# Two graph layers on one core: the order of work where layer two begins is changed

## The chip, the core and the metric

One core of a Trainium2 chip runs the whole program in one launch. The core has five engines that run their own instruction streams and meet at semaphores: TensorE (PE, matrix products and transposes), VectorE (DVE), ScalarE (ACT), GpSimd (POOL) and SyncE (SP), which here only issues DMAs. The metric is the device time of one execution in microseconds; lower is better. The kernel before took 3624.22 us (median of 3 runs, 3620.76 to 3637.07).

## The reference, cut to what matters

There are N = 2708 nodes with D = 512 features, and a dense adjacency matrix `adj` of N x N zeros and ones.

```python
# layer one: normalise, clear, graph attention with 8 heads of 64, add
h = relu(layernorm(x))
x = x + relu(gat(h, adj))
# layer two: normalise, clear, two diffusion steps, add
X = relu(layernorm(x))
S = adj + I;  Rf = S / rowsum(S);  Rb = S / colsum(S)[:, None]
Xf = Xb = Xa = X;  Z = 0
for s in range(2):
    logits = Xa @ W1 @ W2 @ (Xa @ W3).T          # N x N
    A = softmax(logits, only the largest entries of a row that reach mass 0.9)
    Xf = Rf @ Xf;  Xb = Rb @ Xb;  Xa = A @ Xa
    Z = Z + Xf @ U1[s] + Xb @ U2[s] + Xa @ U3[s]
out = x + layernorm(X + Z)
```

In step one (s = 0) Xf and Xb are still both X, so one product with S serves both: S.T-tiles times X, scaled by row sums for Xf and by column sums for Xb. In step two they differ.

## The kernel before

**Tiles.** The 2708 nodes are 22 tiles of 128 rows, the last of 20 rows. Tiles go in 11 pairs (G = 2; the text calls a pair also a group), in 6 quads, and the columns of a row of logits in 6 chunks of 452. `early_tiles` is 18: the tiles ahead of the last two pairs.

**Layer one** (lines 202 to 464) works through six column blocks of adj. For each block and head, DVE makes a masked weight tile `e` (L440) and PE multiplies it (L442). A block's tiles are then finished by `finished`, in stages: turn the heads' sums (L351), share them out, normalise, clear (`v`, L390), and `asked`: transpose v (L397), project it to keys and queries (`project`, L160, which writes kq_d through POOL), and split v into two parts for exact products (`split_rows`, which writes vhl_d through POOL). Stages of earlier blocks are threaded through the next block's loop; those of the last three tiles (19, 20, 21) come at the very end, with nothing beside them. Here `rest` also writes `xb_d`, the input of the last sum. While layer one runs, S is written to DRAM as `s_d`. After layer one some small tiles are set up, among them `ones`, `across` and `below_d` (L500 to L505, the pool `ramps`), on the addresses that layer one has left, and after them the pool `big` on the same base, with `va` (the values X, 22 tiles) and `keys`.

**Layer two, step one**, is the loop over s = 0 from L950. From L1235 on the order of PE, ACT, DVE and SP is the order of the program (`manual_schedule`), so each of these engines works strictly through its list; POOL's order is made by a scheduler. Per pair of tiles:

- `Logits.queries` loads q, `Logits.products` makes two rows of logits p (L536 on PE, L538 copies by ACT). p has 4 buffers: two pairs.
- `Logits.exp` holds the maxima (L564, DVE), two exponentials a tile on ACT, and six looks a tile (ACT passes over p that measure the mass above a guess, L571).
- `search` (DVE) finds the cut for mass 0.9: passes over p (L650), then `finish` (L844, L846, L779), which writes the kept weights `keep` and a flag that picks a branch (L928). `early` and `late` are hooks: what is called there stands at that place in each engine's list. `early` begins with the outstanding `pending` splits and the next pair's maxima.
- `attended` (PE) transposes keep (L1096), ACT copies it (L1100), and PE multiplies it with va (L1118). Its twelve steps take work from two lists: `fills` (ACT's passes for a later pair) and `others` (a part of S's block).
- `mixed` multiplies with U3 (L1158) and projects for step two (L160).

**S's blocks.** `part(half, b)` gives the steps of half a block for one quad: an even b is 22 `product` steps (load hl of vhl_d, 512 KB, and s_r of s_d, 256 KB, then eight matmuls, L1012); an odd b is `across` (four copies to `tt`, also stored as tt_d for step two), then four `through` steps with U1 (L1030, each loads a u_k) and a `scaled` that puts x tiles on the list `pending` for `split_rows` to fhl_d, and the same with U2 for bhl_d. hl, s_r and u_k have 3 buffers each.

**The opening before.** SP loads keys in two pieces (L965), then q; PE makes the logits of pair 0; then all of part 0 (22 products); then va is loaded (L976). For g = -1: part 1 and pair 1's logits, while DVE searches pair 0. From g = 0 on, phase g holds part g + 2, pair g + 2's logits, the attention of pair g and the search of pair g + 1. Parts end with part 11, so phase 10 of step one has none. At g = 0 the ACT passes left over from the opening (`looks`) are threaded into `attended` first.

**Step two** has the same loop with its own parts (L1009), which also load tt_d back (L1000).

Of the kernel before, what the change touches and what calls it, by code (L numbers as in the profile page):

```python
# [53 lines left out]
def kernel(  # L54
# [41 lines left out]
    const = ctx.enter_context(tc.tile_pool(name="const", bufs=1))  # L96

# [104 lines left out]
    with ExitStack() as l0:  # L202
# [133 lines left out]
        def finished(t, o_t, c0, bank, final):  # L336
# [48 lines left out]
            def cleared():  # L385
                _, o, mean, rs = held
                v = work.tile([P, D], F32, name="v", bufs=3)
                held.append(v)
                nc.vector.tensor_scalar(o[:pr], o[:pr], mean, rs, op0=OP.subtract, op1=OP.mult)
                nc.scalar.activation(v[:pr], o[:pr], AF.Relu)  # L390
                nc.gpsimd.dma_start(out=va_d[cols[t], :], in_=v[:pr])

            def asked():
# [6 lines left out]
                if not final:  # L400
                    split_rows(halves, nc.gpsimd, v[:pr], t, vhl_d)
                project(halves, bank(1), v_t, t, 0, bufs=TG)

            def rest():
                split_rows(halves, nc.vector, held[4][:pr], t, vhl_d)
                with_beta(held[0])

            return [turned, shared, normed, cleared, asked] + [rest] * final

        later = {}  # L410
        for ci, tiles in enumerate(tchunks):
# [95 lines left out]
    class Logits:  # L507
# [20 lines left out]
        def products(self):  # L528
            wide, small, ps_l = self.pools
            for q, t in zip(self.q, self.grp):  # L530
                pr = rows[t]
                p = wide.tile([P, N], F32, name="p", bufs=4)
                for c0, c1 in chunks:
# [5 lines left out]
                self.p.append(p)  # L539
# [402 lines left out]
    big = ctx.enter_context(tc.tile_pool(name="big", bufs=1))  # L942
    va = big.tile([P, NT, D], F32, name="va")

    keys = big.tile([P, N], F32R, name="keys")
# [4 lines left out]
    for s in range(STEPS):  # L950
        last = s == STEPS - 1
        with ExitStack() as st:
# [5 lines left out]
            small = st.enter_context(tc.tile_pool(name=f"s{s}small", bufs=2, reuse_waits="tile"))  # L958
            ps_t = st.enter_context(tc.tile_pool(name=f"s{s}pst", bufs=2, space=PSUM, reuse_waits="tile"))
            ps_a = st.enter_context(tc.tile_pool(name=f"s{s}psa", bufs=2, space=PSUM, reuse_waits="tile"))  # L960
            ps_s = st.enter_context(tc.tile_pool(name=f"s{s}pss", bufs=1, space=PSUM, reuse_waits="tile"))

            def asked(s, c):
                for i in range(2):
                    nc.sync.dma_start(out=keys[i * DA:(i + 1) * DA, c].bitcast(F32), in_=kq_d[s][:DA, i, c])  # L965

            if not last:
                asked(s, slice(0, early_tiles * P))
            asked(s, slice(early_tiles * P, N))
            if last:  # L970
                also = st.enter_context(tc.tile_pool(name="s1also", bufs=1))
            rank = also.tile([P, N], BF16, name="rank") if last else None

            def values(queue):
                for t in range(NT):
                    queue.dma_start(out=va[:rows[t], t, :], in_=(xa_d if last else va_d)[cols[t], :])  # L976

# [4 lines left out]
            def part(half, b):  # L982
# [12 lines left out]
                def product(c):  # L995
                    if c == 0:
                        half[:] = [ps_s.tile([P, D], F32, name=f"q{i}") for i in range(len(quad) if last else KD)]
                        if last and first:
                            across_t.append(work.tile([P, KD, 2 * G * P], F32, name="tt", bufs=1))
                            nc.sync.dma_start(out=across_t[-1][:, :, :w], in_=tt_d[b // 2][:, :, :w])  # L1000
# [14 lines left out]
                def across():  # L1015

                    tt = work.tile([P, KD, 2 * G * P], F32, name="tt", bufs=1)
                    for k in range(KD):
                        nc.scalar.copy(tt[:, k, :w], half[k][:, :w])
                    nc.gpsimd.dma_start(out=tt_d[b // 2][:, :, :w], in_=tt[:, :, :w])  # L1020
                    across_t.append(tt)

                def through(u, k, start):
# [5 lines left out]
                    for j in range(len(quad)):  # L1029
                        nc.tensor.matmul(half[j], lhsT=across_t[-1][:, k, j * P:(j + 1) * P], rhs=u_k,  # L1030
                                         start=(start and k == 0), stop=(start and k == KD - 1))

                def scaled(inv, to, now):

                    paced(pending, len(pending))
                    for j, t in enumerate(quad):
                        pr = rows[t]
                        x = work.tile([P, D], F32, name="xe", bufs=4)
# [31 lines left out]
                for u, inv, to, now in ((u1[1], rinv, fhl_d, b > 1), (u2[1], cinv, bhl_d, False)):  # L1070
                    steps += [lambda k=k, u=u: through(u, k, True) for k in range(KD)]
                    steps.append(lambda inv=inv, to=to, now=now: scaled(inv, to, now))
# [162 lines left out]
            with tc.manual_schedule(engines={PE, ACT, DVE, SP}):  # L1235
                junk = wide.tile([P, -(-N // 4) * 2], F32, name="junk", bufs=1)
                lg = [Logits(pools, s, grp, keys, rank) for grp in pairs[:1]]
                lg[0].queries()
                lg[0].products()
                steps = lg[0].exp(looks=False)  # L1240
                counts = []
                if last:
                    values(nc.gpsimd)
                    heads, counts = ranked(junk.bitcast(BF16)[:, :N], list(range(early_tiles, NT)), "keep", 2)
                    paced(heads, len(heads))
                for step in lg[0].maxima + steps + counts:
                    step()
                half = []
                lg += [Logits(pools, s, grp, keys, rank) for grp in pairs[1:2]]
                lg[1].queries()  # L1250
                others = part(half, 0)
                if last:
                    paced(others, NT // 2)
                    spread()
                    lg[1].products()
                paced(others, len(others))
                if not last:
                    values(nc.sync)
                done = []
                ready = None  # L1260
                looks, left = [], []
                for g in range(-1, NP):
# [3 lines left out]
                    others = part(half, g + 2)  # L1266
                    if g + 2 < NP and not (last and g < 0):
# [106 lines left out]
```

## Time and profile before

| | us |
|---|---|
| median of 3 runs | 3624.22 |
| the profiled execution | 3630.61 |
| its span | 3628.7 |
| PE busy | 3334.1 (92% of the span) |
| DVE busy | 2652.9 (73%) |
| ACT busy | 1505.5 (41%) |
| layer one's last L442 matmul ends | 1051.8 |
| first logits of layer two begin (L536) | 1089.4 |
| group 2's logits resume (L536) | 1221.6 |
| step two's products begin (L1009) | 2342.5 |

All durations and instants in this text are those of the profiled execution, counted from the start of its span, and its own time is 6.4 us above the median of the runs. In a row of the time line the first two numbers are start and length; a bracket at the end tells how long the engine stood idle before it and what released it. A row of the waits reads: who waited, for whom, us in total, times, longest.

### The profile page before, as it was taken

The numbers are of one execution on the slowest core, as the hardware profiler recorded it, in microseconds if no ns is written. First come the engines' busy times: TensorE is split into PE (matmuls) and PEld (weight loads), VectorE is DVE, ScalarE is ACT, GpSimd is POOL, SyncE is SP. The second block draws the span as 40 slices with busy tenths as digits, with TensorE's granted clock in tenths as the row PEclk, the third lists the DMA queues.
The fourth block names the chain that finished last, engine by engine and source line by source line (L and its number), as shares of the span: only waits on it lengthen the run. The fifth ranks groups of instructions, "written<-read, shape, count | busy, mean of one in ns | idle before, by whom it ended". The sixth has DMA issues, their size and how long they took to land. (4 is left out here: it accounts for less than half of the span.)

```text
span 3628.7 us, 34073 instructions
## 1 busy us (share of the span) xinstructions
PE 3334.1 (92%) x10797; PEld 1718.8 (47%) x10797; DVE 2652.9 (73%) x4828; ACT 1505.5 (41%) x2269; POOL 854.2 (24%) x1054
## 2 busy tenths in 40 slices
PE   7999999998967789999999999889999999999877
PEld 4433333333444454555546454355555555555433
DVE  4587888889975455546365463598889988889984
ACT  2344212011103566656465662335545654455610
POOL 4114241515321021122222221221112212122211
PEclk9999999999989889999999999999999999999989
DMA  3477424232218352534445253574556445565433
GB/s 114 150 242 246 149 89 143 75 118 94 94 59 283 116 186 90 211 108 163 160 151 192 95 205 109 172 275 159 201 186 231 151 164 203 185 224 191 160 119 132
DMA packets 247956, 579.99 MB, mean 160 GB/s; under 512 B 33305, under 2 KB 67049, under 8 KB 243491
## 3 DMA queue, kind: packets, MB, share of 16 engines
q1 hardware_dynamic: 226695, 503.59, 41.4%
q0 software_dynamic: 21040, 73.88, 5.3%
q8 instruction: 86, 1.41, 0.2%
q14 instruction: 135, 1.11, 0.1%
HBM read 471.68 MB, written 105.68 MB: 159 GB/s over the span
## 5 line engine op out<-in xcount | busy, mean ns | idle before, releaser
L1118 PE MATMUL a<-va,at 128*128 128x512 f32 (+2 forms) x1936 | 893.6, 601 | 8.4 <-ACT at L1100 8.3
L442 PE MATMUL po<-e,fw 128*65 128x512 f32 (+4 forms) x2112 | 842.7, 554 | 30.7 <-DVE e L440 21.7
L440 DVE SCALAR_TENSOR_TENSOR e<-r_b,kk,a_c 128x512 f32<-128x512 f32 (+4 forms) x1056 | 750.8, 739 | 71.6 <-PE po L442 21.6
L571 ACT ACTIVATE junk_a<-p,nth 128x2708 uint8<-128x2708 f32 (+1 forms) x240 | 612.7, 2553 | 57.8 <-POOL nth L586 53.5
L1009 PE MATMUL q<-hl,s_r 128*128 128x512 f32 x1936 | 525.9, 420 | 66.9 <-DMA s_r<-s_d 65.1
L442 PEld LDWEIGHTS po<-e,fw 128*65 128x65 f32 (+1 forms) x2112 | 286.9, 140 | 546.6 <-issue 270.9
L1118 PEld LDWEIGHTS a<-va,at 128*128 128x128 f32 (+2 forms) x1936 | 340.3, 187 | 381.1 <-issue 336.5
L1009 PEld LDWEIGHTS q<-hl,s_r 128*128 128x128 f32 x1936 | 363.1, 191 | 219.7 <-issue 59.7
L650 DVE SCALAR_TENSOR_TENSOR junk<-p,th 128x2708 bf16<-128x2708 f32 (+1 forms) x132 | 424.6, 3217 | 3.3
L1100 ACT COPY at<-t 128x512 f32<-128x512 f32 (+3 forms) x308 | 140.0, 476 | 503.9 <-PE t L1096 499.6
L1030 PE MATMUL q<-u_k,tt 128*128 128x512 f32 x704 | 318.6, 595 | 10.3 <-DMA u_k<-in_L_gnn_U_dram 10.3
L1012 PE MATMUL q<-s_r,hl 128*128 128x512 f32 (+1 forms) x1056 | 280.6, 410 | 11.6 <-DMA s_r<-s_d 11.3
L538 ACT COPY p<-t 128x452 f32<-128x452 f32 (+2 forms) x264 | 130.8, 536 | 382.6 <-PE t L536 332.8
L1012 PEld LDWEIGHTS q<-s_r,hl 128*128 128x128 f32 x1056 | 186.7, 188 | 99.6 <-issue 51.5
L1030 PEld LDWEIGHTS q<-u_k,tt 128*128 128x128 f32 x704 | 134.1, 191 | 160.8 <-issue 145.7
L536 PE MATMUL t<-keys,q_t 128*128 128x452 f32 x528 | 155.5, 419 | 58.6 <-ACT p L538 45.4
L564 DVE TENSOR_REDUCE nmx<-p 128x1 f32<-128x2708 f32 (+1 forms) x44 | 130.6, 2968 | 104.4 <-ACT p L538 104.4
L846 DVE MAX8 vn<-keep 128x8 f32<-128x2708 f32 (+1 forms) x66 | 196.8, 2981 | 2.3
L424 ACT ACTIVATE s_c<-a_c 128x512 fp32r<-128x512 f32 (+3 forms) x132 | 76.2, 577 | 249.5 <-DMA a_c<-in_adj_t_dram 122.0
L1096 PE MATMUL t<-ident,keep 128*128 128x128 f32 (+1 forms) x968 | 147.8, 275 | 29.4 <-DVEq L933 13.9
L1096 PEld LDWEIGHTS t<-ident,keep 128*128 128x128 f32 (+1 forms) x968 | 115.0, 140 | 121.8 <-issue 86.6
L1158 PE MATMUL a<-u_k,v_t 128*128 128x512 f32 (+1 forms) x352 | 168.4, 615 | 1.8 <-DMA u_k<-in_L_gnn_U_dram 1.5
(312 smaller groups left out, 3308.2 us busy)
## 6 DMA issues: line engine op xcount, KB each, us to landing
s_r<-s_d SPq DMA_DIRECT2D x330, 256.0 KB
hl<-vhl_d SPq DMA_DIRECT2D x132, 512.0 KB
hl<-fhl_d SPq DMA_DIRECT2D x132, 512.0 KB
hl<-bhl_d SPq DMA_DIRECT2D x132, 512.0 KB
u_k<-in_L_gnn_U_dram SPq DMA_DIRECT2D x184, 256.0 KB
arow<-in_adj_dram SPq DMA_DIRECT2D x21, 1354.0 KB
s_d<-s_c SPq DMA_DIRECT2D x88, 256.0 KB
a_c<-in_adj_t_dram SPq DMA_DIRECT2D x84, 256.0 KB
```

Source lines behind the costliest of these rows:

```text
L440: nc.vector.scalar_tensor_tensor(e[:pr, :cw], r_b[:pr, i, :cw], kk[:pr, t, hd:hd + 1], a_c[t][:pr, :cw], op0=OP.max, op1=OP.mult)
L442: nc.tensor.matmul(po[i][:, :cw], lhsT=fw[:pr, t, hd, :], rhs=e[:pr, :cw], start=(t == 0), stop=(t == NT - 1))
L536: nc.tensor.matmul(pl[:, :c1 - c0], lhsT=q[:, i], rhs=self.keys[:, c0:c1], start=(i == 0), stop=(i == 1))
L571: nc.scalar.activation(junk[:pr], self.p[i][:pr], func, **kw)
L650: nc.vector.scalar_tensor_tensor(self.junk_b[:pr], p, th, p, op0=OP.is_ge, op1=OP.mult, accum_out=dst)
L846: v.max(vs, keep[0][:pr])
L1009: nc.tensor.matmul(half[j], lhsT=s_r[:, j * P:(j + 1) * P], rhs=hl[:, h], start=(c == 0 and h == 0), stop=(c == NT - 1 and h == 1))
L1012: nc.tensor.matmul(half[j][:, :w], lhsT=hl[:, h, j * P:(j + 1) * P], rhs=s_r[:, :w], start=(c == 0 and h == 0), stop=(c == NT - 1 and h == 1))
L1030: nc.tensor.matmul(half[j], lhsT=across_t[-1][:, k, j * P:(j + 1) * P], rhs=u_k, start=(start and k == 0), stop=(start and k == KD - 1))
L1096: nc.tensor.transpose(pt[:rows[c], j, :pr], keep[i][:pr, cols[c]], ident[:pr, :pr])
L1118: nc.tensor.matmul(pa[:pr], lhsT=at[:rows[c], j, :pr], rhs=va[:rows[c], c, :], start=(c == 0), stop=(c == NT - 1))
L1158: nc.tensor.matmul(pz[i][:rows[t]], lhsT=v_t[i][:, k, :rows[t]], rhs=u_k, start=(k == 0), stop=(k == KD - 1))
```

## The change

What it does, in the order of the program:

1. A pool `turn` with four 2 KB tiles named `v` is opened first. Layer one's v comes from it, and later the four parts of `tt`, which become tiles of their own; tt_d is written and read in four DMAs, one for each part.
2. The last three tiles of layer one are no longer projected and split there. They are put on a list `unasked`.
3. `big` waits tile by tile instead of for whole pools, and `keys` is its first tile. In the step's pools the PSUM of S's products is taken first.
4. Step one opens with three products of part 0. Then, three times: a third of the first 18 tiles' keys (SP), one product, and the split, transposition and projection of one of the unasked tiles. The keys of the last tiles are loaded by POOL's queue.
5. The logits of pair 0 come in two parts, the five chunks that need no late keys first, with three products between them and the last chunk. Then 9 products, pair 1's logits, the last 4 products, part 1 with the loads of va between its steps, and the whole of part 2.
6. From then on phase g holds part g + 3 instead of g + 2, so phases 9 and 10 have none. The splits of part 1 are held back until after the first search, and the ACT passes of pair 1 are all issued in the opening, instead of being threaded through phase 0.
7. Step two keeps its order; only the four tt tiles and the pools concern it.

The diff, cut to its core:

```diff
+    turn = ctx.enter_context(tc.tile_pool(name="turn", bufs=4, reuse_waits="tile"))
...
-                v = work.tile([P, D], F32, name="v", bufs=3)
+                v = turn.tile([P, D], F32, name="v")
...
-                if not final:
-                    split_rows(halves, nc.gpsimd, v[:pr], t, vhl_d)
-                project(halves, bank(1), v_t, t, 0, bufs=TG)
+                split_rows(halves, nc.gpsimd, v[:pr], t, vhl_d)
+                project(halves, bank(1), v_t, t, 0, bufs=2)
             def rest():
-                split_rows(halves, nc.vector, held[4][:pr], t, vhl_d)
                 with_beta(held[0])
-            return [turned, shared, normed, cleared, asked] + [rest] * final
+                unasked.append((t, held[4]))
+            return [turned, shared, normed, cleared, rest if final else asked]
...
-        def products(self):
+        def products(self, cs=chunks):
...
-    big = ctx.enter_context(tc.tile_pool(name="big", bufs=1))
+    big = ctx.enter_context(tc.tile_pool(name="big", bufs=1, reuse_waits="tile"))
+    keys = big.tile([P, N], F32R, name="keys")
     va = big.tile([P, NT, D], F32, name="va")
-    keys = big.tile([P, N], F32R, name="keys")
...
-            if not last:
-                asked(s, slice(0, early_tiles * P))
-            asked(s, slice(early_tiles * P, N))
...
-                            across_t.append(work.tile([P, KD, 2 * G * P], F32, name="tt", bufs=1))
-                            nc.sync.dma_start(out=across_t[-1][:, :, :w], in_=tt_d[b // 2][:, :, :w])
+                            across_t.append([turn.tile([P, D], F32, name="v") for _ in range(KD)])
+                            for k, tt in enumerate(across_t[-1]):
+                                nc.sync.dma_start(out=tt[:, :w], in_=tt_d[b // 2][:, k, :w])
...
-                    paced(pending, len(pending))
+                    if b > 1:
+                        paced(pending, len(pending))
...
+                    paced(others, 3)
+                    for n, (t, v) in enumerate(unasked):
+                        asked(s, slice(n * early_tiles // len(unasked) * P, (n + 1) * early_tiles // len(unasked) * P))
+                        paced(others, 1)
+                        split_rows(parts, nc.vector, v[:rows[t]], t, vhl_d)
+                        v_t = transposed(up, ps_t, v, rows[t], "v_t")
+                        project(small, ps_t.tile([P, 512], F32, name="t"), v_t, t, s)
+                    asked(s, slice(early_tiles * P, N), nc.gpsimd)
+                    lg[0].queries()
+                    lg[1].queries()
+                    ahead = [c for c in chunks if c[1] <= early_tiles * P]
+                    lg[0].products(ahead)
+                    paced(others, 3)
+                    lg[0].products(chunks[len(ahead):])
+                    steps = lg[0].exp(looks=False)
+                    for step in lg[0].maxima + steps:
+                        step()
+                    paced(others, 9)
+                    lg[1].products()
+                    paced(others, len(others))
+                    others = part(half, 1)
+                    loads = values(nc.sync)
+                    while others:
+                        paced(others, 1)
+                        paced(loads, 2)
+                    others = part(half, 2)
+                    paced(others, len(others))
...
-                    others = part(half, g + 2)
-                    if g + 2 < NP and not (last and g < 0):
+                    if last or g >= 0:
+                        others = part(half, g + 2 if last else g + 3)
+                    if 0 <= g < NP - 2:
                         lg[g + 2].products()
...
-                            paced(pending, len(pending))
+                            if g >= 0:
+                                paced(pending, len(pending))
...
+                        paced(fills, len(fills))
                         if last:
-                            paced(fills, len(fills))
                             paced(others, len(others))
-                        else:
-                            paced(others, 1)
-                            paced(fills, 2 * G + 1)
-                            while others:
-                                paced(others, KD + 1)
-                                paced(fills, G)
-                        looks.extend(fills)
...
+                        if g < 0 and not last:
+                            paced(pending, len(pending))
```

## The prediction

> **What bounds the kernel now.** I read the page first: engine totals and the forty slices. The profiled execution took 3630.61 us, with a span of 3628.7; slices of 90.7 us.
>
> ```profile
> PE 3334.1 (92%) x10797; PEld 1718.8 (47%) x10797; DVE 2652.9 (73%) x4828; ACT 1505.5 (41%) x2269; POOL 854.2 (24%) x1054
> ...
> PE   7999999998967789999999999889999999999877
> ...
> PEclk9999999999989889999999999999999999999989
> ```
>
> TensorE (PE) is busy nearly everywhere; the hole is in slices 12 to 14, from about 1000 to 1360 us, where layer two begins. The busy time by stretch, cut where PE's work changes kind, is the second view (stretch, length, busy time of each engine, granted clock, DMA share, GB/s):
>
> ```profile
> 1052.00:1089.40 37.40, 9.04 (x60) 7.63 (x58) 18.66 (x48) 4.52 (x13) 19.75 (x32) 0.55 0.41 124
> 1089.40:1153.50 64.10, 52.85 (x201) 36.35 (x202) 36.77 (x63) 17.10 (x22) 6.75 (x9) 0.97 0.85 294
> 1153.50:1171.40 17.90, 6.59 (x26) 3.60 (x24) 13.38 (x18) 13.93 (x23) 0.66 (x1) 0.82 1.01 364
> ...
> 1201.90:1221.60 19.70, 0.00 (x0) 0.00 (x0) 14.78 (x42) 5.63 (x6) 0.00 (x0) 0.61 0.07 29
> ...
> 1449.60:1558.90 109.30, 107.80 (x391) 66.15 (x390) 65.36 (x142) 60.39 (x74) 26.23 (x32) 1.00 0.62 219
> 1558.90:1659.50 100.60, 96.12 (x278) 46.10 (x276) 47.84 (x103) 65.03 (x83) 14.87 (x30) 0.97 0.24 83
> 2173.40:2249.00 75.60, 74.58 (x229) 36.02 (x227) 36.87 (x77) 15.67 (x35) 13.93 (x22) 1.00 0.34 110
> ```
>
> The first four rows are the transition. The last three are pair phases of step one: 96 to 99% PE, with VectorE (DVE) at 65 or less. So in step one PE is the bound, its work only moves, and the change is worth the PE idle time that it removes between 1052 and 1450. Third view, what PE's matmuls waited for from 1052 to 1222:
>
> ```profile
> PE t L536 <- ACT p L538: 20.8, 6, 19.8
> PE t L536 <- DMA q_t<-kq_d: 12.5, 1, 12.5
> PE po L397 <- ACT v L390: 12.1, 1, 12.1
> PE q L1012 <- DMA s_r<-s_d: 10.9, 14, 1.4
> PE q L1030 <- DMA u_k<-in_L_gnn_U_dram: 10.3, 1, 10.3
> PE po L160 <- ACT v_t L399: 3.7, 3, 2.6
> ```
>
> That is 70 us, each line one cause: layer one's last normalisation, the key and query round trip, S's products short of data, u_k queued behind va, and group 2's logits waiting for buffers that DVE's search of group 0 holds. After 1222 two waits follow, of 8.4 us (1281, the row below) and 6.3 us (1344, behind ScalarE's looks), and about 2 us is lost after each long one to a halved clock. Call it 95 us. The fourth view is the order of time:
>
> ```profile
> 1094.91 2.97 DVE L564 TENSOR_REDUCE nmx<-p 128x1 f32<-128x2708 f32 x1 [9.85 <-ACT p L538]
> ...
> 1221.06 0.17 DVE L939 RECIPROCAL rden<-den 128x2 f32<-128x2 f32 x1 [3.64 <-DVEq L928]
> ...
> 1289.34 1.12 PE L1096 MATMUL t<-ident,keep 128*128 128x128 f32 x4 [8.36 <-ACT v_t L149]
> ```
>
> The search of group 0 takes 126.2 us between the first two rows. 12.4 of it is a wait for group 1's logits; 22 (1171.3 to 1193.4) is S's first `split_rows`, queued ahead of `finish` and waiting for `xe`. Without them it takes 92. The last view is the SP queue's own waits:
>
> ```profile
> SPq L965 <- DVE below_d L505: 76.5, 1, 76.5
> ```
>
> SP could have issued long before. It stood at the first key load until 1071.9, because `big` lies where the ramps' tiles lay.
>
> **Part by part: the start.** After the last transposes (1054.2) PE now goes to S's products. Their SBUF lies under layer one's last e tiles, free with the last matmul at 1051.8; 4 us from issue to use (bounds: tt's 3.2 at least, and 4.5 for the first product of before, issue 1093.4 to start 1097.9) puts product 0 at 1056. One product loads 786 kB; 22 took 55.6 us, 2.53 each, or 311 GB/s. Products 0 to 2 end at 1063.
>
> Next on SP is the first piece of keys. With keys first in `big`, it still lies on the ramps' tiles, tile-by-tile waits or not, and L505 depends on the same normalisation as before. I keep 1072. Behind it on SP stand product 3's loads and all later ones; who waits is PE. The Trainium skill, "DMA: Bandwidth & Descriptors", section "Anatomy of one DMA", says that a semaphore wait happens on the issuing sequencer ahead of dispatch. That speaks against this order: product 3 has nothing to do with keys, yet stands behind them. The row of 76.5 us is such a standing queue. By the rule, product 3 has its data at 1078 (issue 1073.5, 4.5 more beside 0.39 MB of keys), 15 us of idle PE; were the queue to flow, the data would be there at 1066 and everything below comes 12 us sooner. I take the rule.
>
> Then three rounds of a key piece, a product and a projection. PE per round: a product 1.9, four transposes 0.7, the v_t copy 0.6 with its hand-over, eight L160 1.1, some of it at half clock: 5 us, 1094 at the end. DVE's three splits (1.1 each) and the POOL work were there before. The third key piece goes on POOL's queue behind kq_d's writes (3.1 us median to land): keys complete at about 1105. Meanwhile PE does ten chunks of logits (8.8 for twelve: 7.3; 1101.5) and products 6 to 8 (1107); the two last chunks end at 1108.5. **The search of group 0 so starts at 1108, 13 us later than before.**
>
> Products 9 to 17 are short of data (2.53 each against 1.9 of PE): 1129. Group 1's logits, 8 us: 1137, before DVE asks for them at 1108 + 50 = 1158. Products 18 to 21: 1145. Across, four copies: 1147.5. The two through-passes, 29.7 before with 2 us of half clock, plus 1 for eviction: 1176; u_k and va, 0.8 MB a step of 3.6 us, now alternate and hide, so the 10.3 us wait goes.
>
> **Block 2 in the opening.** 22 products more, three preloaded: 7 us, 18 × 2.53 and 2 at the end make 1230.5. Eight deferred splits write 4.2 MB of fhl and bhl once the search ends (1200), in the same stretch: 0 to 13.5 us at 311 GB/s; nearest to the full overlap, I take 9. Group 2's logits start at **1239**. By the same page's Specifications (358 GB/s from HBM for a core) a product loads in 2.2 and this would be 1233. The row of 294 GB/s holds only S's loads, so I keep 2.53.
>
> Hidden beside it, and what a late one costs: the search ends at 1200 and its buffers are free; eight splits take DVE to about 1218 (four took 8.8); ScalarE's four exponentials and twelve looks of group 1, at 2.7 each with the points between, run 1177 to 1226. All lie under 1239, by 13 us; beyond that each us is paid.
>
> **The loop.** Phase 0 now carries block 3 (row of 100.6), phase 1 block 4 (row of 109.3): group 2's phase starts at 1239 + 209.9 = 1448.9. Before, it started at 1449.6, with one block less behind it. What is that block worth? Phase 9 (last row, 75.6) held half a through-pass (16 × 2 instructions, 14.3) and no logits (7.5): a bare phase is 68.8, so an even block costs 40.5 on PE. Difference: 1448.9 − 1449.6 − 40.5 = **−41.2 us**.
>
> **The tail.** Phase 9 loses its filler. DVE needs 57 us there against 61 of bare PE: cover is left, 0 to 5 us lost, I take 0. In step two, tt comes in four loads of 2 kB rows for one: three SP issues of 0.4 more, six times, 0 to 7 us where PE stands; SP is idle between products, so 0. Pool moves, kq buffers 4 to 2 (16 us between uses against 3.1 to land) and PSUM order: nothing.
>
> Sum: 3630.6 − 41 = 3589.4 on the profiled execution. That lies 6.4 above the median of 3624.22, so **3583** beside the median. 0.5% (18 us) is about what a measurement here can tell from no change.
>
> **Rivals.** (1) *The queue flows*: L505 runs early, or keys don't wait for it. For it: nothing of keys is needed by product 3. Against: the 76.5 us row. 12 us more: 3571. (2) *DVE and ScalarE take over the opening*: the late search pushes looks and group 1's keep past PE. Slack is 13 us; a search 30 us later than 1108 costs 17, with 4 in phase 9: 3604. For it: the keys now end a chain of five queues. Against: DVE is under two thirds busy. (3) *The idle time only moves*, and group 2 starts at 1280: no change, 3624. (4) *Slower: two S blocks and va back to back outrun the DMA engines.* The opening moves 34.6 (S) + 5.6 (va) + 2.1 (u_k) + 1.9 (keys, queries) + 5.3 MB (writes) = 49.4 MB; at 311 GB/s that is 159 us, 1054 to 1213. To cost 0.5%, group 2 must start after 1298: 202 GB/s or less. The rows of 294 and 364 speak against; narrow key and query rows for. At 190 GB/s: 1314 and 3658.
>
> **From cases to numbers.** Likeliest 0.55, with its own range 3568 to 3598 (product 0 and the 4 us, 0 to 13.5 us of writes, 0 to 12 of the tail); rival 1 0.15; rival 2 0.20, a third of it above 3606; rival 3 0.05; rival 4 0.05. Faster by over 0.5% (below 3606): 0.55 + 0.15 + 0.14 = 0.84; within 0.11; slower 0.05. Range 3560 to 3608: it leaves out the best of rival 1, the worst of rival 2, and rivals 3 and 4.
>
> **What would show it.** Right: L1012 on PE from 1056; a PE gap of 10 to 16 us before product 3 whose chain leads through SP to L505; the first `nmx` near 1108; no L1030 wait for u_k; no wait on L538 before group 2; group 2's logits near 1239; phases after it of 101 and 109 in turn; phase 9 near 61. Wrong: no such gap (rival 1), PE waiting for `keep` or L538 in phases 0 and 1 (rival 2), GB/s below 220 in the opening (rival 4), or phases longer than before, which no step here allows for.

## The result, and the profile after

The changed kernel took **3583.47 us** (median of 4 runs, 3580.31 to 3586.98) beside 3627.88 us for the kernel before on the same chip (4 runs, 3620.76 to 3637.07): a ratio of 0.9876, 95% interval 0.985 to 0.9903. The forecast was 3583. The profiled execution took 3586.98 us with a span of 3585.1, which is 43.6 less than the profiled execution before.

The rows of the page that answer to those of before (engine totals, then PE and its granted clock in forty slices):

```profile
PE 3326.5 (93%) x10797; PEld 1718.2 (48%) x10797; DVE 2657.5 (74%) x4828; ACT 1502.8 (42%) x2269; POOL 858.4 (24%) x1074
...
PE   7998999998988799999999999889999999999977
...
PEclk9999999999999999999999999999999999999989
```

PE's busy time is hardly less (3334.1 before): no work has gone, only idle time. The hole in slices 12 to 14 has gone from 6, 7, 7 to 8, 8, 7: shallower, and not closed. The windows show what is left. Columns as before: stretch, length, busy time of PE, its weight loads, DVE, ACT and POOL, granted clock, DMA share, GB/s.

```profile
1052.00:1092.70 40.70, 20.61 (x98) 15.77 (x95) 18.43 (x47) 4.17 (x10) 16.78 (x26) 0.75 0.72 229
1092.70:1131.20 38.50, 31.66 (x122) 22.64 (x122) 11.17 (x5) 17.47 (x24) 10.80 (x18) 0.96 0.79 271
1131.20:1148.00 16.80, 14.23 (x58) 9.54 (x56) 16.04 (x35) 7.90 (x16) 1.31 (x3) 1.00 0.58 196
1148.00:1175.70 27.70, 27.70 (x65) 12.40 (x66) 26.63 (x45) 4.81 (x7) 0.97 (x2) 1.00 0.96 348
1175.70:1241.80 66.10, 48.02 (x176) 34.89 (x176) 36.63 (x94) 43.21 (x35) 12.34 (x20) 0.93 0.87 308
1451.00:1560.30 109.30, 103.55 (x302) 50.02 (x300) 56.13 (x115) 71.43 (x96) 23.03 (x37) 0.97 0.31 100
1560.30:1661.30 101.00, 100.76 (x365) 62.42 (x365) 55.23 (x126) 54.09 (x61) 20.26 (x28) 1.00 0.62 210
2151.60:2212.80 61.20, 60.13 (x190) 29.33 (x189) 43.77 (x88) 12.12 (x26) 12.98 (x17) 1.00 0.25 76
```

The rows are, in order: the start, to the first logits; then the logits of pair 0 with products; pair 1's logits and products; the through-passes of block 1, where PE has no idle time at all; block 2, 22 products in 66.1 us with 48.0 of PE. The last three are two phases of step one, as long as before, and phase 9, now bare: 61.2.

What PE waited for from layer one's end to group 2's logits (who, for whom, us in total, times, longest):

```profile
PE q L1013 <- DMA s_r<-s_d: 38.0, 19, 14.0
PE t L538 <- DMA keys<-kq_d: 2.8, 1, 2.8
PE q L1013 <- DVE o L366: 2.8, 1, 2.8
PE t L161 <- ACT v_t L150: 1.8, 3, 0.7
PE t L538 <- ACT p L540: 1.0, 5, 0.2
PE q L1030 <- ACT v L1020: 0.8, 1, 0.8
```

Some 47 us stand where 70 stood, although the stretch now holds a whole block more. The waits for q, for v, for u_k and for group 2's buffers are gone. One wait of 14.0 leads the list, and SP's own waits name what is behind it:

```profile
SPq L965 <- DVE below_d L506: 16.0, 1, 16.0
```

In order of time (start, length, instruction, idle time before and its releaser), for PE first and then DVE:

```profile
1078.71 1.22 PE L1013 MATMUL q<-s_r,hl 128*128 128x512 f32 x2 [14.05 <-DMA s_r<-s_d]
```

```profile
1108.65 2.97 DVE L565 TENSOR_REDUCE nmx<-p 128x1 f32<-128x2708 f32 x1 [25.41 <-ACT p L540]
...
1202.07 0.17 DVE L940 RECIPROCAL rden<-den 128x2 f32<-128x2 f32 x1 [6.19 <-DVEq L929]
```

Product 3 starts 14.05 us after product 2, and the search of group 0 runs from 1108.65 to 1202.07, 93.4 us. Since layer one itself ends between 1046 and 1052 from one execution to the next, instants below are counted from the end of its last loop matmul (L443) where several kernels are set side by side:

| from L443's end, us | group 2's logits | start of `attended` of phase 1 | step two's first product |
|---|---|---|---|
| changed kernel | 190.7 | 298.9 | 1255.9 |
| changed kernel, run again | 186.9 | 294.8 | 1249.1 |

### The profile page after: what moved, and what is told of

It is laid out like the page before. It is cut to its first block, busy times and chain, and to the rows that moved or that the text cites. A ratio compares the mean times of both kernels' runs of the same rounds, so it can differ in the third digit from the quotient of the medians.

```text
span 3585.1 us, 34134 instructions
## 1 busy us (share of the span) xinstructions
PE 3326.5 (93%) x10797; PEld 1718.2 (48%) x10797; DVE 2657.5 (74%) x4828; ACT 1502.8 (42%) x2269; POOL 858.4 (24%) x1074
## 5 line engine op out<-in xcount | busy, mean ns | idle before, releaser
L1120 PE MATMUL a<-va,at 128*128 128x512 f32 (+2 forms) x1936 | 893.4, 601 | 10.4 <-ACT at L1102 10.3
L443 PE MATMUL po<-e,fw 128*65 128x512 f32 (+4 forms) x2112 | 838.1, 552 | 35.6 <-DVE e L441 21.3
L443 PEld LDWEIGHTS po<-e,fw 128*65 128x65 f32 (+1 forms) x2112 | 286.2, 139 | 547.5 <-issue 269.1
L1102 ACT COPY at<-t 128x512 f32<-128x512 f32 (+3 forms) x308 | 139.9, 475 | 496.9 <-PE t L1098 492.9
L1013 PE MATMUL q<-s_r,hl 128*128 128x512 f32 (+1 forms) x1056 | 282.2, 415 | 41.4 <-DMA s_r<-s_d 38.4
L1030 PE MATMUL q<-u_k,v 128*128 128x512 f32 x704 | 318.4, 595 | 0.8 <-ACT v L1020 0.8
L1013 PEld LDWEIGHTS q<-s_r,hl 128*128 128x128 f32 x1056 | 193.3, 195 | 124.0 <-issue 56.5
L1030 PEld LDWEIGHTS q<-u_k,v 128*128 128x128 f32 x704 | 134.0, 190 | 150.8 <-issue 145.5
```

The source lines that it names most:

```text
L443: nc.tensor.matmul(po[i][:, :cw], lhsT=fw[:pr, t, hd, :], rhs=e[:pr, :cw], start=(t == 0), stop=(t == NT - 1))
L1013: nc.tensor.matmul(half[j][:, :w], lhsT=hl[:, h, j * P:(j + 1) * P], rhs=s_r[:, :w], start=(c == 0 and h == 0), stop=(c == NT - 1 and h == 1))
L1030: nc.tensor.matmul(half[j], lhsT=across_t[-1][k][:, j * P:(j + 1) * P], rhs=u_k, start=(start and k == 0), stop=(start and k == KD - 1))
L1120: nc.tensor.matmul(pa[:pr], lhsT=at[:rows[c], j, :pr], rhs=va[:rows[c], c, :], start=(c == 0), stop=(c == NT - 1))
```

## The experiments

All times are medians; the ratio is to the kernel before, run beside them (medians 3626 to 3629 us). A difference between two kernels is worth only what the intervals leave of it: half an interval is some 0.002, or 7 us, so that two ratios tell kernels apart from about 8 to 10 us on. The instants from traces are those of one execution each.

**The changed kernel once more**, as the measure for the others.

> The changed kernel once more, for a second profile and a closer ratio: step one has 35 us less than before at its end, step two 9 us less, and only the first was forecast. Theory (step two's 9 us are the four tt loads or something else that the change does): step two again takes some 1275 us from its first product to the end, against 1286 before. Rival (step two differs from one execution to the next): a figure nearer 1286. Ratio 0.985 to 0.990.

3586.84 us (3574.68 to 3593.36), ratio 0.9883 [0.9862, 0.9905]. In this execution step two's first product stands at 2301.3, which is 41.2 before the 2342.5 of the kernel before; step two then takes 1286.4 (1286.2 before). In the first execution of the same kernel these are 35.6 sooner and 1278.2. Step two's length differs by 8 us between executions of the same code, so the 8 us that the first pair of profiles shows there can't be put down to the change.

**The four parts of tt alone**, put into the kernel before.

```diff
-                            across_t.append(work.tile([P, KD, 2 * G * P], F32, name="tt", bufs=1))
-                            nc.sync.dma_start(out=across_t[-1][:, :, :w], in_=tt_d[b // 2][:, :, :w])
+                            across_t.append([work.tile([P, D], F32, name="tt", bufs=KD) for _ in range(KD)])
+                            for k, tt in enumerate(across_t[-1]):
+                                nc.sync.dma_start(out=tt[:, :w], in_=tt_d[b // 2][:, k, :w])
...
-                    nc.gpsimd.dma_start(out=tt_d[b // 2][:, :, :w], in_=tt[:, :, :w])
...
+                        nc.gpsimd.dma_start(out=tt_d[b // 2][:, k, :w], in_=tt[:, :w])
```

> The kernel before with one part of the change alone: tt in four tiles, stored and loaded in four DMAs. Theory (this makes step two's 9 us): step two takes 1277 us instead of 1286, time 0.9975 of before. Rival (the term is nothing, as forecast, and the 9 us differ between executions): ratio 0.999 to 1.001, step two's length anywhere between.

3628.8 us, ratio 1.0006 [0.9997, 1.0016], step two 1286.8 us. The term of 0 to 7 us for three more SP issues is nothing, as taken.

**The ramps aside.** The two small tiles of the pool `ramps`, `ones` and `across`, go to the other end of SBUF, so that `keys` no longer lies on them. (`below_d` itself is a tile of `const`; its line, L506, is the last that reads `across`, and so the one that `keys` waits for.)

```diff
-    with tc.tile_pool(name="ramps", bufs=1) as pool:
+    with tc.tile_pool(name="ramps", bufs=1, side="right") as pool:
```

> The two small ramps tiles are put at the other end of SBUF, so the first key load no longer waits for them and SP flows. Theory (keys standing at the head of SP's queue cost 12 us): the gap of 14 us before product 3 falls to 4 or less, the first nmx comes near 1097 instead of 1108.7, group 2's logits near 1230 instead of 1241.8, time 12 us below the changed kernel's (3571). Rival (the idle time only moves, into the DMA-bound block 2 or the split writes): the gap goes, group 2's logits stay within 3 us of 1242, time 3580 to 3587.

3578.04 us, ratio 0.9874 [0.9846, 0.9902]. L506 now runs at 11.6 us instead of 1069.2, SP issues the first load of keys at 1052.8 instead of 1069.5 with no wait for below_d, and the idle time before product 3 is 0.52 us. PE's waits:

```profile
PE q L1013 <- DMA s_r<-s_d: 24.3, 22, 2.4
PE t L161 <- ACT v_t L150: 6.1, 3, 5.0
PE t L538 <- ACT kq_b L167: 2.6, 1, 2.6
```

The first `nmx` comes at 50.4 after L443's end (57.6 in the changed kernel, 54.1 run again), group 2's logits at 178.9 (190.7, 186.9). So the 14 us gap was the queue. Up to the first search 4 to 7 us of it are won, since 5.0 came back as a wait for ACT's copy v_t, which the longer wait had covered. ACT's rows show what held the copy (its transposes had ended at 1067.3):

```profile
1069.80 0.63 ACT L391 ACTIVATE v<-o 20x512 f32<-20x512 f32 x1 [1.55 <-DVE o L390]
1071.63 0.59 ACT L150 COPY v_t<-t 128x512 f32<-128x512 f32 x1 [1.20 <-DMA xb_d<-xt]
```

Most of it is ACT's own list, in which layer one's last normalisation (L391) stands ahead of the copy; 1.2 us is the buffer's address, on which a store of layer one had still to end. At the start of group 2's logits the gain is 8 to 12, because block 2 too ran in 61.9 us instead of 66.2; why it did, this run does not show. By the medians it is 5 to 9 us, but the ratio differs from that of the changed kernel beside it (0.9883) by less than the intervals: the times of this run alone don't show it.

**v_t aside as well.**

```diff
-  v_t = transposed(up, ps_t, v, rows[t], "v_t")
+  v_t = transposed(work, ps_t, v, rows[t], "at")
```

> The ramps stand aside, as in the first experiment, and v_t of the three unasked tiles is a buffer on layer one's o tiles no longer: it lies where `at` lies, free once layer one's loop has ended. My theory: the first experiment gained 10 to 12 us where the queue was freed and gave 5 us back to a new wait (PE for v_t, 5.0 us at 1067), so without it the three rounds end 4 to 5 us sooner, group 2's logits begin about 175 us after layer one's last matmul of its loop (178.9 in the first experiment, 187 to 191 in the changed kernel), and the time is 3574. Rival: products 3 to 5 are by then paced by their loads (2.5 us each), not by PE, and take the 5 us back: 179 us and 3578 as in the first experiment.

3575.26 us, ratio 0.9859 [0.984, 0.9877]. PE's waits over the same stretch:

```profile
PE q L1013 <- DMA s_r<-s_d: 22.9, 18, 3.1
PE t L161 <- ACT at L150: 4.8, 3, 3.8
PE t L538 <- ACT kq_b L167: 4.7, 1, 4.7
```

The long wait shrinks by the 1.2 us of the address, to 3.8: the copy now follows L391 at once, at 1070.45, but still follows it. What is saved turns up one step on, at the first logits, which wait for the projection's copies (L167). Group 2's logits begin at 180.8: no sooner than with the ramps alone. The rival was right as to the trace. It named the loads; what the trace shows is the chain of v, v_t and the projection's copies. The median lies between the theory's 3574 and the rival's 3578 and can't decide.

**The same cure for the kernel before.**

```diff
-    with tc.tile_pool(name="ramps", bufs=1) as pool:
+    with tc.tile_pool(name="ramps", bufs=1, side="right") as pool:
```

> The kernel before with the ramps aside and nothing else. The wait of 76.5 us at the head of SP's queue was the row on which the forecast of the 15 us gap rests. My theory: it costs time only where work that doesn't need the keys stands behind it, as S's products do in the changed kernel; in the kernel before, PE at that place waits for q and for the keys of the last tiles, which come from layer one's last projection whatever the queue does. So 0 to 4 us less: 3623 to 3627. Rival: the standing queue itself was the hole of the kernel before: then the first logits come 10 us or more sooner, and the time is 3615 or less.

3627.19 us, ratio 0.9994 [0.9983, 1.0004]: nothing. SP's waits of this kernel show the queue standing at the same line for other things:

```profile
SPq L965 <- DVE o L369: 65.0, 1, 65.0
...
SPq L965 <- DMA kq_d<-kq_hl: 16.7, 1, 16.7
SPq L965 <- POOL xt L382: 7.4, 1, 7.4
```

and PE waits 12.4 us for q_t as it did. A wait at the head of a queue costs what stands behind it; in the kernel before that was nothing that could have run, in the changed kernel it is S's products.

**Not one block ahead.** Part 2 stays in phase 0; the opening is otherwise the changed one.

```diff
-                    others = part(half, 2)
-                    paced(others, len(others))
...
-                        others = part(half, g + 2 if last else g + 3)
+                        others = part(half, g + 2)
```

> The new opening, but S's blocks not one ahead: block 2 is not in the opening and phase g holds part g + 2 as before. Theory (what block 2 fills is the time in which PE would wait for the search and the looks): group 2's logits wait for ScalarE's looks and start near 1228, only 14 us sooner than with block 2; then a phase of 109 and one of 101, and the time is 23 to 28 us above the changed kernel's, 3606 to 3612. Rival (the opening alone brings the gain, the block ahead is only work moved): group 2's logits near 1190 and 3580 to 3590.

3607.91 us, ratio 0.9944 [0.9923, 0.9964], as expected. PE came to group 2's logits at 1173 and stood until 1223.4:

```profile
1223.41 2.87 PE L538 MATMUL t<-keys,q_t 128*128 128x452 f32 x6 [48.59 <-ACT p L540]
```

Without the block ahead the time is 21 to 24 us above the changed kernel's, and still 19 below the kernel before. So somewhat less than half of the gain is the start with S's products, and the rest is the block that fills the 48.6 us in which ScalarE still works through group 1's passes, up to 1222.75, and only then copies group 2's p. (The search of group 0 had ended at 1197.)

**A later search.** Ten passes more over p in the first search; they change nothing but its length.

```diff
+            for n in range(10 if s == 0 else 0):
+                i, pr = o.tiles[n % 2]
+                o.mass(i, pr, lg.th[:pr, 0, i:i + 1], lg.pts[:pr, 0, 2, i:i + 1])
             for j in range(NA):
```

> Ten more passes over p (3.1 us each) ahead of the first search of step one, so it ends 31 us later; their results are overwritten by the passes that follow. The prediction put the slack at 13 us: time 17 us above the changed kernel's, about 3603. Rival (the changed kernel's row for the second search, done at 1326 for a use at 1350, leaves more room): group 2's logits stay at 1240 and the time is at most 6 us above, 3583 to 3593.

3592.93 us, ratio 0.9917 [0.9897, 0.9936]. The search ended 176 us after L443's end (151 and 145 in the two executions of the changed kernel). PE's waits (its added lines push L1013 to L1016):

```profile
PE q L1016 <- DMA s_r<-s_d: 29.6, 22, 13.4
PE t L538 <- ACT p L540: 15.0, 6, 14.1
```

PE stood 14.1 us for the buffers of p, as rival 2 of the prediction has it. Yet phase 1 starts 298.9 after L443's end, no later than in the changed kernel's first execution and 4.1 later than in its second; step two's first product comes at 1255.8, 0 to 7 later. The medians say 6 to 9 us, the ratios 12 to 15 with some 10 either way, so the times don't exclude the 17 us of rival 2. In the trace most of PE's wait is paid back by block 2, which ran in 54.2 us instead of 66.2. The eight splits follow the search, so their writes now came behind it; the next experiment tells how much of the 12 us is theirs.

```profile
1168.30:1222.50 54.20, 44.31 (x177) 31.40 (x177) 48.10 (x103) 29.04 (x24) 6.68 (x9) 1.00 0.83 289
```

**The splits later.** Here the writes leave block 2 without a later search.

```diff
                         ready = search(lg[g + 1], opened, junk, early, late)
-                        if g < 0 and not last:
-                            paced(pending, len(pending))
```

> The changed kernel with one thing different: the eight splits of part 1 are not made right after the first search but at the start of the next one's early hook, in phase 0; the ramps are where they were. My theory, from block 2, whose products took 2.9 us each while 4.2 MB of splits were written beside them: without the writes they take 2.5 and group 2's logits begin 177 to 181 us after layer one's last loop matmul, 10 us sooner than in the changed kernel; DVE then has 18 to 29 us more in phase 0, where it has some 36 to spare, so that phases 0 and 1 stay at 100 and 109 us: 3577. Rival one: DVE's delay comes to PE in phase 0 or 1 (a wait for `keep` or for L538 of 5 to 15 us): 3582 to 3590. Rival two: the loads are no faster without the writes: 187 to 191 us and 3586.

3590.05 us, ratio 0.9886 [0.9869, 0.9903]. Block 2 alone:

```profile
1174.30:1234.50 60.20, 47.29 (x176) 34.68 (x176) 27.80 (x78) 43.21 (x35) 7.50 (x12) 0.93 0.80 265
```

60.2 us, 6 less than in both executions of the changed kernel, and group 2's logits begin at 182.3 (4.6 to 8.4 sooner). Phase 1 starts at 291.2 (3.6 to 7.7 sooner), without a new PE wait in phase 0. The whole time shows none of this: step two took 1287.6 us in the profiled execution, and the medians can't tell the two kernels apart. In the seven executions that have the writes in block 2 it takes 61.9 to 66.2 us, in the three that don't 54.2 to 60.2. The nearest pair, v_t aside and the next experiment, which differ in this edit alone and ran on the same chip, has 62.6 and 58.0. So the writes cost block 2 some 5 to 6 us. The later search gained 12 there: it moved as many bytes in block 2 as this run (289 GB/s for 54.2 us, 265 for 60.2), so that its other 6 us are not the writes', and what they are is open. That leaving the writes out there makes a faster kernel is not shown.

**All three edits together.**

> All three edits together: ramps aside, v_t aside, the eight splits in phase 0. My theory: they act in different places (the queue at 1055 to 1078, PE at 1067, the DMA engines at 1185 to 1240) and add up: 12 + 4 + 10 us less than the changed kernel where group 2's logits begin (165 us after layer one's last loop matmul), and a time of 3564. Rival: with the start freed the opening is bound by its 311 GB/s of loads throughout, so that the second half of the sum is smaller: 172 us and 3572, or the search of group 0, which starts 12 us sooner and no more, becomes the bound (a PE wait for L538 before group 2): 3570.

3577.05 us, ratio 0.9852 [0.9838, 0.9865]. Group 2's logits begin at 177.4, where the sum said 165 and the rival 172: the parts don't add up. The through-passes end 119.4 after L443's end (124.6 and 120.7 in the changed kernel), so that the start gives 1 to 5 us of its 16, and block 2 takes 58.0, 8 less. It is the lowest ratio here, but the intervals of the three kernels with the ramps aside overlap. Their medians are 5 to 12 us below those of the changed kernel and some 50 below the kernel before; which of the three is best is open. Against the splits later alone, run beside it (0.9886 [0.9869, 0.9903]), the intervals stand apart: here the ramps and v_t aside are worth 13 us by the medians and 12 by the ratios, 8 either way. This is where the times themselves show most clearly that the two edits at the start pay.

**The logits of pair 0 in one piece**, after products 6 to 8.

```diff
-                    ahead = [c for c in chunks if c[1] <= early_tiles * P]
-                    lg[0].products(ahead)
                     paced(others, 3)
-                    lg[0].products(chunks[len(ahead):])
+                    lg[0].products()
```

> The first pair's logits in one part, after products 6 to 8 and all the keys. Theory (the first part fills the time until the last keys land): PE waits some 5 us more for keys, the first nmx comes 4 to 6 us later, near 1113, group 2's logits 3 to 6 us later, time 3586 to 3592. Rival (the split is worth nothing, since S's loads set the pace there): nmx and group 2's logits within 2 us of the changed kernel's.

3586.15 us, ratio 0.989 [0.9872, 0.9908]. The first `nmx` comes at 56.9 (57.6 and 54.1), group 2's logits at 193.4 (190.7 and 186.9). The two parts are worth 3 to 6 us at group 2's logits, as the theory has it, but nothing to 3 at the first `nmx`, and nothing that the medians show.

**The last tiles projected in layer one again**, with S's products and the block ahead kept.

```diff
-                unasked.append((t, held[4]))
...
-            return [turned, shared, normed, cleared, rest if final else asked]
+            return [turned, shared, normed, cleared, asked] + [rest] * final
...
-                        split_rows(parts, nc.vector, v[:rows[t]], t, vhl_d)
-                        v_t = transposed(up, ps_t, v, rows[t], "v_t")
-                        project(small, ps_t.tile([P, 512], F32, name="t"), v_t, t, s)
```

> The last three tiles are projected and split in layer one again; the rest as in the changed kernel. Theory (the projections between the products bring little as long as SP stands at the keys until 1070, since PE then waits there instead): products start near 1077, no gap before product 3 longer than 5 us, the first logits near 1093 as in the changed kernel, group 2's logits within 4 us of 1240, time 3583 to 3590. Rival (the whole wait for the last normalisation, 20 us, comes back): group 2's logits near 1260, time 3600 to 3607.

3596.02 us, ratio 0.9927 [0.9907, 0.9947]. The old wait for v is back, now ahead of all of S's products:

```profile
PE po L398 <- ACT v L391: 12.9, 1, 12.9
PE po L161 <- ACT v_t L400: 3.7, 3, 2.6
```

9 to 13 us by the medians, 16 to 19 by the ratios (some 10 either way), 3 to 9 by the start of group 2's logits and of phase 1. That is more than expected, and the times don't exclude the rival's 3600 to 3607. Products 0 to 2, whose data had landed, run only from 1078.2 (1054.0 in the changed kernel), and product 3's loads wait for their buffers (L1003 is L1002 in this kernel):

```profile
SPq L1002 <- PE q L1012: 10.6, 2, 10.2
```

**All of va ahead of part 1** on SP's queue.

```diff
-                    loads = values(nc.sync)
-                    while others:
-                        paced(others, 1)
-                        paced(loads, 2)
+                    for load in values(nc.sync):
+                        load()
+                    paced(others, len(others))
```

> All loads of va ahead of part 1, as before, instead of two between its steps. Theory (u_k then stands behind 5.6 MB): PE waits 9 to 11 us for the first u_k, group 2's logits 9 to 12 us later, time 3593 to 3598. Rival (the opening is bound by bytes, their order is no matter): group 2's logits within 3 us.

3607.33 us, ratio 0.9948 [0.9929, 0.9968].

```profile
PE q L1030 <- DMA u_k<-in_L_gnn_U_dram: 17.4, 1, 17.4
```

The wait for u_k is back and longer than the 10.3 us of before, and group 2's logits begin at 209.6, 19 to 23 later. The direction is as expected, the size double. The wait itself is 17.4; another 2.5 is the clock, which stays at 0.50 for 20.5 us from 1149.87 on, so that the through-passes take 30.2 us where the changed kernel needs 27.7:

```profile
1165.28:1195.50 30.22, 30.22 (x65) 13.33 (x66) 27.40 (x57) 4.81 (x7) 0.00 (x0) 0.92 0.37 123
```

Taken back one at a time, the projections, the block ahead and the order of these loads cost 9 to 13, 21 to 24 and 21 to 24 us by the medians. That is more than the 40 to 44 of the whole change: they are not separate shares of it. Not tried alone are the tile-by-tile waits of `big`, POOL's queue for the last keys, two instead of four buffers for kq, and the order of the PSUM pools.

## Why the prediction was right, step by step

**The start.** Product 0 was put at 1056; PE issued its first matmul at 1054.04 and then waited 2.8 us for a PSUM bank that DVE still read (the row with o, L366). Products 0 to 2 ended at 1064.7 (forecast 1063). The bank's wait was in no term; the products ended 1.7 us late.

**The standing queue** was the step with most to lose, taken as 15 us of idle PE. It was 14.05, with SP waiting 16.0 us for L506 (below_d). The rule of the Trainium skill that stood behind it ("DMA: Bandwidth & Descriptors", section "Anatomy of one DMA": the semaphore wait is the issuing sequencer's) agrees with that row, and the ramps put aside show its price: rival 1, "the queue flows", was to come 12 us sooner; the kernel in which it flows comes 4 to 7 sooner at the first search and 8 to 12 at group 2's logits, 4 of which are block 2's and not explained. Rival 1 was false of this kernel, and its size was near, though ACT's list ahead of v_t stood in no step. One reading was too simple: of the kernel before, the prediction says that SP could have issued long before. With the ramps aside there it still stands 65.0 us at that line, for o.

**Keys, first logits, first search.** The three rounds ended at 1092.7 (1094), the first search began at 1108.65 (1108) and ended at 1202.07 (1200).

**Pair 1 and the through-passes.** 1131.2 to 1138.8 (1129 to 1137) and 27.7 us (27.7). The wait of 10.3 for u_k has gone, and the experiment with va first shows that taking va and u_k in turn is what took it away.

**Block 2.** With the writes 63.5 us were forecast and 66.1 measured. The parts were less good than the sum: without writes 54.5 was forecast and 58 to 60 measured where only the splits were moved (54.2 with the later search), and the writes, put at 9 out of 0 to 13.5, cost 5 to 6. The two errors in part cancel, which is luck. The row of 294 GB/s, which the prediction takes to hold only S's loads, holds loads of va too; the 2.53 us don't rest on it, they are read from the products themselves. Group 2's logits began at 1241.8 for 1239, and in the second execution at 1239.1.

**The cover of block 2.** DVE's eight splits were to end at 1218 by scaling four of before (8.8 us); they ended at 1231. DVE stood for the writes of earlier splits in between:

```profile
1211.13 0.43 DVE L182 TENSOR_SCALAR split_hl<-xe 128x512 int32<-128x512 int32 x1 [6.75 <-DMA fhl_d<-split_hl]
...
1219.34 0.43 DVE L182 TENSOR_SCALAR split_hl<-yo 128x512 int32<-128x512 int32 x1 [4.53 <-DMA fhl_d<-split_hl]
...
1228.40 0.43 DVE L182 TENSOR_SCALAR split_hl<-yo 128x512 int32<-128x512 int32 x1 [5.57 <-DMA bhl_d<-split_hl]
```

This step was wrong by 13 us; the slack that was left swallowed it, and phase 0 shows no wait for it.

**The loop and the tail.** From group 2's logits to those of phase 2, 209.2 us (209.9); phase 9 61.2 (61). Phase 7 took 96.8 us in this execution and 92.9 in the second one: PE had a gap of 2.98 us there for ACT's copy (L1102), which no step had. In the other kernels with the block ahead it takes 93.1 to 93.5 or 96.5 to 97.7; what decides between the two is open.

**The sum.** The forecast was −41.2 at step two's first product. Measured: −35.6 in the first execution (2.8 us at group 2's logits and 3 in phase 7 are the difference) and −41.2 in the second. Step two was to gain nothing; it gave 8.0 in the first pair of profiles and −0.2 in the second. That the median came out at the forecast itself is in part luck. The forecast was 41.2 below a median of 3624.22 for the kernel before; the kernel before that ran beside the changed one had 3627.88, and the gain was 44.4, or 40.3 where the changed kernel was run again.

**Rival 2** was not this kernel: no wait for p stood before group 2. Its mechanism exists (14.1 us of PE for p after a search 31 us later). The trace shows 0 to 7 us of its 17 at step two's first product, since block 2 ran 12 us faster, 5 to 6 of them without the writes that a late search pushes back; the times leave 17 possible. **Rivals 3 and 4**: group 2 started at 1242, not 1280 or 1314, and the five stretches before it moved 279 GB/s on the mean of their lengths, where rival 4 needed 202 or less.

## What to carry to other kernels

Before a step is moved ahead of another, look at the head of each in-order queue that it passes: here a wait at the head was free as long as nothing that could run stood behind it, and cost up to its length once something did (16.0 us of SP, 14.05 of PE). What holds it can be an address alone: keys lay where two small tiles lay, and these were written late because they in turn lay on layer one's addresses. Moved aside, they were written at 11.6 us. When one wait is taken away, expect the next to keep a part of it: of the 14 us only 4 to 7 were won up to the first search; 5.0 went to a wait for the copy v_t, which stood in ACT's list, in order too, behind layer one's last normalisation.

## What the runs showed that was not expected

Between 1082 and 1242 PE was never idle for more than 3 us, and yet the granted clock halved there four times, for 3.4 us each: once in the products of part 0 and three times in block 2. Of the six gaps of 1.9 to 3.0 us in that stretch four were followed by it (those of 1.99, 2.50, 2.73 and 2.96 us; those of 2.34 and 2.83 were not). The first and the last of the four:

```profile
1118.95 7.36 PE L1013 MATMUL q<-s_r,hl 128*128 128x512 f32 x24 [1.99 <-DMA s_r<-s_d]
...
1238.63 3.41 PE L1013 MATMUL q<-s_r,hl 128*128 128x512 f32 x8 [2.96 <-DMA s_r<-s_d]
```

The four dips begin at 1119.55, 1187.82, 1221.95 and 1239.02, which is 20, 10 and 5 steps of 3.41 us apart. Windows laid on these steps tell the dips from the two gaps that did no harm. In order of time: the two steps over the gap of 2.83; the step ahead of the first dip, and that dip; the two steps over the gap of 2.34; the step ahead of the last dip (PE's busy time follows the length, the granted clock is the third number from the end):

```profile
1102.48:1105.90 3.42, 2.09 (x10) 1.40 (x8) 0.00 (x0) 0.00 (x0) 0.00 (x0) 1.00 0.88 285
1105.90:1109.31 3.41, 1.91 (x9) 1.69 (x10) 0.66 (x1) 0.97 (x2) 0.00 (x0) 1.00 0.99 372
...
1116.13:1119.55 3.42, 1.43 (x7) 0.85 (x6) 0.00 (x0) 3.39 (x4) 0.00 (x0) 1.00 0.90 296
1119.55:1122.97 3.42, 3.42 (x10) 2.66 (x9) 0.00 (x0) 3.09 (x4) 0.22 (x1) 0.50 0.46 175
...
1208.30:1211.71 3.41, 2.14 (x8) 1.42 (x8) 0.54 (x2) 3.38 (x3) 0.00 (x0) 1.00 1.03 411
1211.71:1215.13 3.42, 2.07 (x8) 1.43 (x9) 1.70 (x3) 3.35 (x5) 0.36 (x1) 1.00 0.96 382
...
1235.61:1239.02 3.41, 0.46 (x3) 0.39 (x3) 3.06 (x11) 0.00 (x0) 0.00 (x0) 1.00 0.89 303
```

Ahead of the four dips PE was busy for 0.46 to 1.43 us of a step (13 to 42%). The gaps of 2.83 and 2.34 each fall on two steps, with 1.91 to 2.14 us busy (56 to 63%), and the clock stayed. So in this execution the dips go with how little PE did within one step, and not with the length of the gap; nothing was run to set the two apart.

What the dips cost in a stretch that waits for loads is open. With the ramps aside the clock was 1.00 through block 2, with gaps of up to 2.4 us, and it took 61.9; with v_t aside too it was 0.92, and it took 62.6. That is a difference of less than 1 us. In the later search, at 1.00, block 2 took 54.2, and with the splits later, at 0.93, 60.2; there PE's busy time makes up 3 of the 6 us.
